# Two Mamba scans on one core: one GpSimd product for each pair, softplus' correction moved from VectorE to ScalarE and TensorE, gating in place

## The chip, the cores and the metric

The kernel runs on one core of one Trainium2 chip. The metric is the device time of one execution in microseconds (us); the time before is the median of three runs, 3107.72 us (3107.16 to 3108.42). TensorE is PE in the profile (its weight loads PEld), VectorE DVE, ScalarE ACT, GpSimd POOL, SyncE SP. PSUM is the memory that TensorE writes and ScalarE and VectorE read; SBUF is the working memory of all engines.

## The reference, cut to what matters

Four layers with residuals are applied to an image of 2 x 128 x 56 x 56: an agent attention, a 3x3 convolution, a mixture of experts, and a layer with two Mamba scans, one along each row of 56 positions and one against it. The change touches the last layer alone (and one buffer of the step that leads to it).

```python
def _mamba(x, in_w, conv_w, conv_b, xproj_w, dt_w, dt_b, Alog, Dp, out_w):
    xi, z = jnp.split(x @ in_w.T, 2, axis=-1)
    xc = jax.nn.silu(conv_b + sum((xp[:, k:k + L, :] * conv_w[:, k] for k in range(K))))
    dt, Bm, Cm = jnp.split(xc @ xproj_w.T, [DT_RANK, DT_RANK + D_STATE], axis=-1)
    dt = jax.nn.softplus(dt @ dt_w.T + dt_b)
    A = -jnp.exp(Alog)
    def step(h, inp):                      # 16 states for each of 256 channels
        dA = jnp.exp(dt_l[:, :, None] * A)
        h = dA * h + (dt_l * u_l)[:, :, None] * B_l[:, None, :]
        y = jnp.einsum('bds,bs->bd', h, C_l)
    y = (ys + xc * Dp) * jax.nn.silu(z)
    return y @ out_w.T
fwd = _mamba(xs, ...); bwd = _mamba(xs[:, ::-1, :], ...)[:, ::-1, :]
y = layernorm(jnp.concatenate([fwd, bwd], axis=-1) @ fuse_w.T)
x = x + y
```

## The kernel before, in words

**Blocks, halves and units.** The function mamba_pair cuts the 2 x 3136 positions into 14 blocks of 448 (8 rows). A block has a forward and a backward half (f and b); each half holds 256 channels x 16 states, worked as 8 pairs of units, 16 units in all. One unit is a tile of 128 partitions x 896. So a block is 32 units, and the main loop runs over 14 x 32 = 448 units, one loop step for each.

**One step of the loop**, in program order for every engine:

- `decay` of the next unit: two ScalarE exponentials (line 1820) write dA to PSUM. There are two dA buffers, so the decay of unit n+1 waits until the scan of unit n-1 is done.
- The fetches, ScalarE copies out of PSUM that belong to work booked one step earlier.
- `push` of the unit three ahead: one GpSimd product dBu = dtu2 * B (line 1831, 128 x 896), into one of four dBu buffers.
- `scan` (line 1853): the VectorE recurrence h = dA * h + dBu. After the second unit of a pair, h is multiplied by C: by GpSimd for pairs 0, 3, 6 of f and 0, 3 of b (line 1859, 128 x 1792), by VectorE for the other eleven pairs of the block (line 1862), which then wait for c_ps.
- `close`, when a half is finished: yv = y * zs, the gating by VectorE (line 1879).
- `read_out` (line 1841): TensorE spreads a row of C over partitions, into c_ps, in the single PSUM bank "c".
- `collect` (line 1873): TensorE sums the states of an earlier unit into y. A half's first collect also writes the skip term (line 1869).
- What `book` has put on this step.

**Bookings.** While the units of block n-1 are scanned, block n is prepared. The steps of that preparation are counted from the first unit of block n-1: steps 0 to 15 lie beside its f half, 16 to 31 beside its b half, and steps 32 on are already beside block n's own f half. The order on each engine is the program's (a manual schedule). The line that chooses a PSUM bank is the tag: "mm" or "c", one bank each, so that a matmul group of a tag waits until ScalarE has fetched the group before it. Among the bookings are, for block n: `norm` 6, `f.conv` 7 and 8, silu 10 and 18 (each with two loads of ScalarE's table), `b.conv` 12, `f.low` 15, `f.step` 17 and 20, `f.softplus` 22 (bank "c") and 24, `f.weigh` 25, `f.gate(0)` 26, `f.send_steps` 27, `b.step(0)` 27, `b.softplus` 32 and 33 (both bank "c"), `f.gate(1)` 33, `b.gate(0)` 35, `b.weigh` 38. And for the finished block: `fuse` 36, `measure` 38, `root` and `newton` 39.

**Softplus** is log(1 + exp(-|v|)) + max(v, 0), with a correction for the rounding of 1 + e. For each half and each m of two: `step` lets TensorE write v to dt_ps, and four ScalarE operations follow (lines 1765 to 1769), the last of which writes w = 1 + e back to that bank. `error` (VectorE, line 1775) forms (w - 1) - e. `log` (ScalarE, line 1780) takes ln w into sp_u. `softplus` (line 1785) has TensorE add three terms, ln w, minus the correction and max(v, 0), in sp_ps, and a ScalarE copy (line 1786) brings the sum to dt. `weigh` (line 1793) multiplies it by xc into the buffer of sp_u, and `send_steps` (line 1808) spreads dtu and dt by DMAs from SP's queue to dtu2 and dt2, as the units need them.

Of the kernel before, what the change touches and what calls it, by code (L numbers as in the profile page):

```python
# [8 lines left out]
F32 = mybir.dt.float32  # L9
AF = mybir.ActivationFunctionType  # L10
ALU = mybir.AluOpType
# [6 lines left out]
P = 128  # L18
# [3 lines left out]
BLK = 448  # L22
# [1509 lines left out]
def mamba_pair(net, out, wts, combine):  # L1532
# [5 lines left out]
    tc, nc, a = net.tc, net.nc, net.a  # L1538
# [5 lines left out]
    ways, ln_w, ln_b, both, minus, pads = (  # L1544
        wts.ways,
        wts.ln_w,
        wts.ln_b,
        wts.both,
        wts.minus,
        wts.pads,  # L1550
    )
    with ExitStack() as ctx:
# [7 lines left out]
        def gathered(name):  # L1560

            if name == "g0":
                g = work.tile([P, 2, 2, BLK], F32, name=name, tag="h", bufs=4).rearrange("p m r t -> p (m r t)")
            else:
                g = work.tile([P, 2, BLK], F32, name=name, tag="dBu", bufs=4).rearrange("p r t -> p (r t)")
            return g[:T, :512]

        def wide_bank(name):
# [121 lines left out]
        class Half:  # L1690
# [25 lines left out]
            def gate(self, m):  # L1716
                pm = mm("gate_ps")
                if m == 0:
                    self.zs = work.tile([P, 2, BLK], F32, name="zs", tag=f"zs{self.w.d}", bufs=1 if self.w.d == "f" else 2)
                nc.tensor.matmul(  # L1720
                    rows(pm[:, :BLK]),
                    self.w.gate[:, m, :],
                    self.blk.xn[:, :, K - 1 : K - 1 + HW],
                    start=True,
                    stop=True,
                )
                return lambda: nc.scalar.copy(self.zs[:, m, :], pm[:, :BLK])
# [25 lines left out]
            def step(self, m):  # L1753
                pm = mm("dt_ps")
                nc.tensor.matmul(pm[:, :BLK], self.w.dt_t[:, m, :], self.lo[:R, :], start=True, stop=True)
                if m == 0:
                    self.e = work.tile([P, 2, BLK], F32, name="sp_e", tag="sp_e", bufs=1)
                    self.dt = work.tile([P, 2, BLK], F32, name="dt", tag="dt")
                    self.ue = {}
                self.ue[m] = pm[:, :BLK]  # L1760
                bias = self.w.dt_b[:, m : m + 1]

                def fetch():
                    e = self.e[:, m, :]
                    nc.scalar.activation(e, pm[:, :BLK], AF.Abs, bias=bias)
                    nc.scalar.activation(self.dt[:, m, :], pm[:, :BLK], AF.Relu, bias=bias)
                    nc.scalar.activation(e, e, AF.Exp, scale=-1.0)

                    nc.scalar.activation(pm[:, :BLK], e, AF.Identity, bias=1.0)

                return fetch

            def error(self, m):
                e = self.e[:, m, :]
                nc.vector.scalar_tensor_tensor(e, self.ue[m], 1.0, e, ALU.subtract, ALU.subtract)

            def log(self, m):
                if m == 0:
                    self.u = work.tile([P, 2, BLK], F32, name="sp_u", tag="sp_u", bufs=1)
                nc.scalar.activation(self.u[:, m, :], self.ue[m], AF.Ln)  # L1780

            def softplus(self, m):
                pm = mm("sp_ps")
                for n, (mat, v) in enumerate(((net.ident, self.u), (minus, self.e), (net.ident, self.dt))):
                    nc.tensor.matmul(pm[:, :BLK], mat, v[:, m, :], start=n == 0, stop=n == 2)
                return lambda: nc.scalar.copy(self.dt[:, m, :], pm[:, :BLK])

            def weigh(self, m=None):
# [10 lines left out]
            def send_steps(self, m=None):  # L1799

                some = slice(0, 2) if m is None else slice(m, m + 1)
                if not m:
                    self.dt2 = work.tile([P, 2, 2, BLK], F32, name="dt2", tag="dt2")
                    self.dtu2 = work.tile([P, 2, 2, BLK], F32, name="dtu2", tag="dtu2")
                for to, src, queue in ((self.dtu2, self.dtu, nc.sync), (self.dt2, self.dt, nc.sync if m is None else nc.gpsimd)):
                    for s in range(2):
                        for r in range(2):
                            queue.dma_start(to[s * H : (s + 1) * H, some, r, :], src[r * H : (r + 1) * H, some, :])
# [15 lines left out]
                        scale=self.w.A[:, j, 2 * m + r : 2 * m + r + 1],  # L1824
                    )

            def push(self, u):
                j, m = self.unit(u)
                shape = [P, 2, BLK]
                self.dBu[u] = work.tile(shape, F32, name="dBu", tag="dBu", bufs=4)  # L1830
                nc.gpsimd.tensor_tensor(  # L1831
                    self.dBu[u], self.dtu2[:, m], self.B[:, j, :].unsqueeze(1).to_broadcast(shape), ALU.mult
                )

            def read_out(self, u):
# [7 lines left out]
            def scan(self, u):  # L1843

                j, m = self.unit(u)
                if m == 0:
                    self.hc[j] = work.tile([P, 2, 2, BLK], F32, name="h", tag="h", bufs=4)
                h = self.hc[j]
                hf, bf = (v.rearrange("p r t -> p (r t)") for v in (h[:, m], self.dBu[u]))
                af = self.dA[u][:, : 2 * BLK]  # L1850
                if self.w.d == "b":
                    hf, af, bf = hf[:, ::-1], af[:, ::-1], bf[:, ::-1]
                nc.vector.tensor_tensor_scan(hf, af, bf, 0.0, ALU.mult, ALU.add)  # L1853
                if m == 1:
                    shape = [P, 4, BLK]
                    h4 = h.rearrange("p m r t -> p (m r) t")
                    if self.by_pool(u):
                        c = self.C[:, self.w.pooled.index(j), :].unsqueeze(1).to_broadcast(shape)
                        nc.gpsimd.tensor_tensor(h4, h4, c, ALU.mult)  # L1859
                    else:  # L1860
                        c = self.c_ps[:, :BLK].unsqueeze(1).to_broadcast(shape)
                        nc.vector.tensor_tensor(h4, h4, c, ALU.mult)  # L1862
# [12 lines left out]
                    )  # L1875

            def close(self):
                self.yv = work.tile([P, 2, BLK], F32, name="yv", tag=f"yv{self.w.d}", bufs=1)
                nc.vector.tensor_mul(self.yv, self.y[:, :, :BLK], self.zs)

        def silu(inputs, gates):
# [11 lines left out]
        def book(step, *stages, tag="mm", late=0):  # L1893

            agenda.setdefault(step, []).extend((stage, tag, late) for stage in stages)

        for n, blk in enumerate(blocks):

            f, b = blk.ways
            at = STEPS * (n - 1)  # L1900
            if n == 0:
# [7 lines left out]
                book(at + 9, lambda f=f: f.step(1), tag="c", late=1)  # L1909
                book(at + 9, f.send_low)  # L1910
                for m in range(2):
                    book(at + 10 + m, lambda f=f, m=m: f.error(m))
                    book(at + 10 + m, lambda f=f, m=m: f.log(m))
                    book(at + 11 + m, lambda f=f, m=m: f.softplus(m), tag=("mm", "c")[m])
                    book(at + 12 + m, lambda f=f, m=m: f.weigh(m))
                    book(at + 12 + m, lambda f=f, m=m: f.send_steps(m))
# [4 lines left out]
                book(at + 19, lambda b=b: silu(b, None))  # L1921
                for m in range(2):
                    book(2 + 3 * m, lambda b=b, m=m: b.step(m))
                    book(3 + 3 * m, lambda b=b, m=m: b.error(m))
                    book(4 + 3 * m, lambda b=b, m=m: b.log(m))
                    book(7 + m, lambda b=b, m=m: b.softplus(m))
                book(0, b.low)
# [2 lines left out]
            else:  # L1930
# [8 lines left out]
                book(at + 17, f.send_low)  # L1939
                book(at + 17, lambda f=f: f.step(0))  # L1940
                book(at + 18, lambda b=b, g=before.ways[1]: silu(b, g))
                book(at + 19, lambda f=f: f.error(0))
                book(at + 19, lambda f=f: f.log(0))
                book(at + 20, lambda f=f: f.step(1))
                book(at + 21, lambda f=f: f.error(1))
                book(at + 22, lambda f=f: f.log(1))
                book(at + 22, lambda f=f: f.softplus(0), tag="c")
                book(at + 23, b.low)
# [2 lines left out]
                book(at + 26, lambda f=f: f.gate(0))  # L1951
                book(at + 27, lambda b=b: b.step(0))
                book(at + 27, f.send_steps)
                book(at + 28, lambda b=b: b.error(0))
                book(at + 28, lambda b=b: b.log(0))
                book(at + 29, lambda b=b: b.step(1))
                book(at + 31, lambda b=b: b.error(1))
                book(at + 31, lambda b=b: b.log(1))
                book(at + 32, lambda b=b: b.softplus(0), tag="c")
                book(at + 33, lambda f=f: f.gate(1), late=1)  # L1960
                book(at + 33, lambda b=b: b.softplus(1), tag="c")
                book(at + 33, b.send_low)
                book(at + 35, lambda b=b: b.gate(0))
                book(at + 38, b.weigh)
                book(at + 43, b.send_steps)
                book(at + 46, lambda b=b: b.gate(1), late=1)
# [43 lines left out]
                pass  # L2010
        with tc.manual_schedule(engines={E.PE, E.Activation, E.DVE, E.Pool, E.SP}):
            units[0][0].decay(0)
            for h, u in units[:3]:
                h.push(u)
            for n, (h, u) in enumerate(units):
                if n + 1 < len(units):
                    who, i = units[n + 1]
                    who.decay(i)
                fetch(n)
                if n + 3 < len(units):  # L2020
                    who, i = units[n + 3]
                    who.push(i)
                h.scan(u)
                if done:
                    done.pop().close()
# [117 lines left out]
```

## Time and profile before

| | us |
|---|---|
| median of three runs | 3107.72 |
| profiled execution, its own time | 3104.97 |
| its span | 3103.2 |
| first to last scan (448 units, 14 blocks) | 1736.9 to 3075.4 |
| one block in between, from the third unit pair of a b half to the next (2476.72 to 2571.45) | 94.73 |
| in that block: POOL, DVE, PE, ACT busy | 92.22, 89.88, 85.03, 69.85 |

How to read it: the Mamba part takes 1338 of the span's 3103 us. POOL has the most busy time in it and DVE nearly as much, but both sit idle in places. A share of busy time does not say which of them sets the pace; the waits do. In the timeline, a line gives the start, the length, the engine, the code line, the operation and, in brackets, how long the engine sat idle before it and what ended that.

### The profile page before, as it was taken

Reading aid. Unit: us, or ns where it says so; the run is one execution under the profiler, and the core shown is the slowest. Engines: PE = TensorE matmul, PEld = TensorE weight load, DVE = VectorE, ACT = ScalarE, POOL = GpSimd, SP = SyncE. Lnnn points to the kernel's source line nnn. Section 1 sums busy time; section 2 is a strip of 40 time slices with the busy share of each in tenths; the row PEclk is TensorE's granted clock in tenths of the full one; section 3 lists DMA queues with packets and bytes.
Section 4 is the critical chain, followed back from the end, with each engine's and each line's share of the span. In section 5 each row is a group of like instructions: output and inputs, shape, how many; then the busy total and the mean of one; then the engine's idle time right before and its main releaser. Section 6 shows DMA issues by size and latency. Waiting matters only on the chain. (4 is left out here: it accounts for less than half of the span.)

```text
span 3103.2 us, 34608 instructions
## 1 busy us (share of the span) xinstructions
PE 2821.9 (91%) x12964; PEld 1076.6 (35%) x12964; DVE 2224.9 (72%) x2033; ACT 1758.6 (57%) x2634; POOL 1499.1 (48%) x801
## 2 busy tenths in 40 slices
PE   7999999999898899999996789989899998889885
PEld 3333333332334444444443322333323333233321
DVE  5879999999887111111112699999999999999996
ACT  5778788877641011111111577776677767777764
POOL 3000100100511000000003699999999999999995
PEclk9999999999998899999997888999889899999987
DMA  1000000000011878787773553454444535444440
GB/s 54 1 1 1 1 1 1 1 1 1 1 38 43 317 280 323 286 314 301 298 309 104 115 102 81 91 106 90 93 89 84 112 81 113 90 84 91 95 101 8
DMA packets 133271, 333.65 MB, mean 108 GB/s; under 512 B 20228, under 2 KB 90340, under 8 KB 129492
## 3 DMA queue, kind: packets, MB, share of 16 engines
q1 hardware_dynamic: 111104, 303.96, 34.0%
q0 software_dynamic: 5520, 15.62, 1.6%
q10 hardware_dynamic: 16452, 11.61, 1.2%
q8 instruction: 106, 1.74, 0.2%
q14 instruction: 89, 0.73, 0.1%
HBM read 262.56 MB, written 17.20 MB: 90 GB/s over the span
## 5 line engine op out<-in xcount | busy, mean ns | idle before, releaser
L1831 POOL TENSOR_TENSOR dBu<-dtu,Bs 128x896 f32<-128x896 f32 x448 | 943.6, 2136 | 51.7 <-DVE h L1853 39.1
L1853 DVE TENSOR_TENSOR_SCAN h<-dA,dBu 128x896 f32<-128x896 f32 x448 | 878.7, 2006 | 59.7 <-ACT dA L1820 47.4
L620 ACT ACTIVATE ex<-sc 128x896 f32<-128x896 f32 (+1 forms) x700 | 602.7, 917 | 124.4 <-PE sc L617 113.3
L627 DVE TENSOR_TENSOR ex_sum<-ex_sum,ex 128x1792 f32<-128x1792 f32 (+1 forms) x238 | 492.5, 2069 | 35.2 <-ACT ex L620 21.2
L1873 PE MATMUL y<-h,both 128*64 128x448 f32 x1792 | 469.1, 625 | 16.1 <-POOL h L1859 14.9
L617 PE MATMUL sc<-q,k 32*128 32x448 f32 (+1 forms) x2800 | 403.5, 587 | 3.6 <-ACT ex L620 2.9
L1341 PE MATMUL h_ps<-w,xs_c 128*128 128x512 f32 x896 | 393.4, 597 | 10.3 <-issue 10.3
L1820 ACT ACTIVATE dA<-dt,f_A 128x448 f32<-128x448 f32 x448 | 284.4, 637 | 107.0 <-DVE h L1853 76.4
L635 PE MATMUL av<-ex,va 128*32 128x448 f32 (+1 forms) x2800 | 334.3, 552 | 0.1
L1862 DVE TENSOR_TENSOR h<-h,c_ps 128x1792 f32<-128x1792 f32 x154 | 311.3, 2021 | 26.2 <-PE c_ps L1841 11.5
L582 POOL TENSOR_TENSOR a_e<-a_e,a_inv 112x784 f32<-112x784 f32 x14 | 41.6, 2974 | 583.2 <-ACT ex L620 394.5
L1820 ACT ACTIVATE dA<-dt,b_A 128x448 f32<-128x448 f32 x448 | 283.8, 636 | 66.6 <-DVE h L1853 53.2
L1345 DVE TENSOR_TENSOR he<-h_ps,sg 128x512 f32<-128x512 f32 x56 | 38.5, 691 | 381.8 <-PE h_ps L1341 344.3
L1289 POOL DMA_INDIRECT xr<-xd,whom x28 | 28.1, 1003 | 534.8 <-PE xr_ps L1331 490.1
L1859 POOL TENSOR_TENSOR h<-h,Cs 128x1792 f32<-128x1792 f32 x70 | 279.3, 3990 | 2.5 <-DVE h L1853 2.4
L1841 PE MATMUL c_ps<-low,ident 40*64 40x448 f32 x616 | 172.9, 643 | 89.6 <-DVE h L1862 67.5
L1341 PEld LDWEIGHTS h_ps<-w,xs_c 128*128 128x128 f32 x896 | 169.0, 191 | 218.5 <-issue 202.8
L1873 PEld LDWEIGHTS y<-h,both 128*64 128x64 f32 x1792 | 116.7, 150 | 320.0 <-issue 250.7
L617 PEld LDWEIGHTS sc<-q,k 32*128 32x128 f32 (+1 forms) x2800 | 137.7, 181 | 230.0 <-issue 135.2
L1362 PE MATMUL o_ps<-w,ht 128*128 128x512 f32 x448 | 197.2, 592 | 0.4 <-ACT ht L1357 0.4
L1344 ACT ACTIVATE sg<-h_ps 128x512 f32<-128x512 f32 x56 | 33.4, 597 | 256.0 <-PE h_ps L1341 256.0
L1364 ACT ACTIVATE ot<-o_ps,share 128x512 f32<-128x512 f32 x28 | 19.3, 688 | 278.9 <-PE o_ps L1362 278.9
(334 smaller groups left out, 3057.9 us busy)
## 6 DMA issues: line engine op xcount, KB each, us to landing
w<-in_L_conv_w_dram SPq DMA_DIRECT2D x28, 4096.0 KB, 19.4
w<-in_L_conv_w_dram SPq DMA_DIRECT2D x28, 2048.0 KB, 10.2
Bs<-far SPq DMA_DIRECT2D x56, 896.0 KB, 8.6
dtu<-sp_u SPq DMA_DIRECT2D x108, 224.0 KB, 3.9
dt<-dt SPq DMA_DIRECT2D x108, 224.0 KB, 5.2
Cs<-far SPq DMA_DIRECT2D x140, 112.0 KB, 7.3
os<-ot ACTq DMA_DIRECT2D x28, 256.0 KB, 7.8
xd<-xt SPq DMA_DIRECT2D x14, 224.0 KB, 2.7
```

The source lines that it names most:

```text
L617: nc.tensor.matmul(sc[:size, j, :BLK], self.m.k[rows, at : at + size], self.q[rows, :], start=True, stop=True)
L620: nc.scalar.activation(ex[:size, 2 * g : 2 * g + 2, :], sc[:size, :, :BLK], AF.Exp, scale=scale)
L627: nc.vector.tensor_add(self.total[g][:size], self.total[g][:size], ex[:size])
L635: nc.tensor.matmul(self.av[rows, :BLK], self.m.va[:size, i, rows], self.ex[i][:size, h, :], start=i == 0, stop=i == STEPS - 1,)
L1341: nc.tensor.matmul(h_ps, xc[:, q, :], w1[:, q, f0 : f0 + 512], start=q == 0, stop=q == 3)
L1362: nc.tensor.matmul(o_ps, ht[:, i, :], w2[:, i, :], start=i == 0, stop=i == nj - 1)
L1820: nc.scalar.activation(self.dA[u][:, r * BLK : (r + 1) * BLK], self.dt2[:, m, r, :], AF.Exp, scale=self.w.A[:, j, 2 * m + r : 2 * m + r + 1],)
L1831: nc.gpsimd.tensor_tensor(self.dBu[u], self.dtu2[:, m], self.B[:, j, :].unsqueeze(1).to_broadcast(shape), ALU.mult)
L1853: nc.vector.tensor_tensor_scan(hf, af, bf, 0.0, ALU.mult, ALU.add)
L1859: nc.gpsimd.tensor_tensor(h4, h4, c, ALU.mult)
L1862: nc.vector.tensor_tensor(h4, h4, c, ALU.mult)
L1873: nc.tensor.matmul(self.y[r * H : (r + 1) * H, m, :BLK], both, self.hc[j][:, m, r, :], start=False, stop=j == PAIRS - 1)
```

## The change

Three edits, all in mamba_pair:

- `push` now forms the products of a whole pair in one GpSimd operation of 128 x 1792, four units ahead at every second step, into one of three buffers of twice the size.
- `error` is gone. `log` has a second ScalarE operation that writes w - 1 into a free part of the tile dtu2 (which is now allocated in `step`), and TensorE's sum has four terms: e, minus (w - 1), ln w, max(v, 0).
- `close` writes its product over zs, and yv is no tile of its own. The f half's zs gets two buffers and the b half's one.

Three bookings move: `b.log(0)` from step 28 to 29, `b.step(1)` from 29 to 30, `b.gate(0)` from 35 to 38. The second buffer of the experts' gather before the Mamba part shares the dBu tiles, so there are three of them instead of four.

```diff
             def log(self, m):
                 if m == 0:
                     self.u = work.tile([P, 2, BLK], F32, name="sp_u", tag="sp_u", bufs=1)
                 nc.scalar.activation(self.u[:, m, :], self.ue[m], AF.Ln)
+                nc.scalar.activation(self.dtu2[:, m, 0, :], self.ue[m], AF.Identity, bias=-1.0)
-            def error(self, m):
-                e = self.e[:, m, :]
-                nc.vector.scalar_tensor_tensor(e, self.ue[m], 1.0, e, ALU.subtract, ALU.subtract)
             def softplus(self, m):
                 pm = mm("sp_ps")
-                for n, (mat, v) in enumerate(((net.ident, self.u), (minus, self.e), (net.ident, self.dt))):
-                    nc.tensor.matmul(pm[:, :BLK], mat, v[:, m, :], start=n == 0, stop=n == 2)
+                terms = (
+                    (net.ident, self.e[:, m, :]),
+                    (minus, self.dtu2[:, m, 0, :]),
+                    (net.ident, self.u[:, m, :]),
+                    (net.ident, self.dt[:, m, :]),
+                )
+                for n, (mat, v) in enumerate(terms):
+                    nc.tensor.matmul(pm[:, :BLK], mat, v, start=n == 0, stop=n == 3)
                 return lambda: nc.scalar.copy(self.dt[:, m, :], pm[:, :BLK])
-            def push(self, u):
-                j, m = self.unit(u)
-                shape = [P, 2, BLK]
-                self.dBu[u] = work.tile(shape, F32, name="dBu", tag="dBu", bufs=4)
+            def push(self, j):
+                shape = [P, 4, BLK]
+                self.dBu[j] = work.tile([P, 2, 2, BLK], F32, name="dBu", tag="dBu", bufs=3)
                 nc.gpsimd.tensor_tensor(
-                    self.dBu[u], self.dtu2[:, m], self.B[:, j, :].unsqueeze(1).to_broadcast(shape), ALU.mult
+                    self.dBu[j].rearrange("p m r t -> p (m r) t"),
+                    self.dtu2.rearrange("p m r t -> p (m r) t"),
+                    self.B[:, j, :].unsqueeze(1).to_broadcast(shape),
+                    ALU.mult,
                 )
             def close(self):
-                self.yv = work.tile([P, 2, BLK], F32, name="yv", tag=f"yv{self.w.d}", bufs=1)
+                self.yv = self.zs
                 nc.vector.tensor_mul(self.yv, self.y[:, :, :BLK], self.zs)
...
-                    self.zs = work.tile([P, 2, BLK], F32, name="zs", tag=f"zs{self.w.d}", bufs=1 if self.w.d == "f" else 2)
+                    self.zs = work.tile([P, 2, BLK], F32, name="zs", tag=f"zs{self.w.d}", bufs=2 if self.w.d == "f" else 1)
...
...
-                book(at + 28, lambda b=b: b.error(0))
-                book(at + 28, lambda b=b: b.log(0))
-                book(at + 29, lambda b=b: b.step(1))
-                book(at + 31, lambda b=b: b.error(1))
+                book(at + 29, lambda b=b: b.log(0))
+                book(at + 30, lambda b=b: b.step(1))
                 book(at + 31, lambda b=b: b.log(1))
...
-                book(at + 35, lambda b=b: b.gate(0))
+                book(at + 38, lambda b=b: b.gate(0))
...
-            for h, u in units[:3]:
-                h.push(u)
+            for h, u in units[:4:2]:
+                h.push(u // 2)
...
-                if n + 3 < len(units):
-                    who, i = units[n + 3]
-                    who.push(i)
+                if n % 2 == 0 and n + 4 < len(units):
+                    who, i = units[n + 4]
+                    who.push(i // 2)
```

## The prediction

> **What bounds the kernel now.** I read the page's costliest groups first, then the waits of DVE and POOL over eleven blocks (1928.3 to 2979.9 us), then the timeline of one block. From the page:
>
> ```profile
> L1831 POOL TENSOR_TENSOR dBu<-dtu,Bs 128x896 f32<-128x896 f32 x448 | 943.6, 2136 | 51.7 <-DVE h L1853 39.1
> L1853 DVE TENSOR_TENSOR_SCAN h<-dA,dBu 128x896 f32<-128x896 f32 x448 | 878.7, 2006 | 59.7 <-ACT dA L1820 47.4
> L1859 POOL TENSOR_TENSOR h<-h,Cs 128x1792 f32<-128x1792 f32 x70 | 279.3, 3990 | 2.5 <-DVE h L1853 2.4
> ```
>
> POOL is the busiest, but its idle time ends with a scan of DVE, and DVE's with a dA of ACT. The waits over eleven blocks (total us, times, longest):
>
> ```profile
> DVE h L1853 <- ACT dA L1820: 38.3, 34, 2.0
> DVE h L1862 <- PE c_ps L1841: 5.0, 11, 0.9
> POOL dBu L1831 <- DVE h L1853: 27.3, 32, 1.9
> ```
>
> No scan waits for POOL there; POOL waits for DVE to free a dBu buffer. So the pace is DVE's chain with ACT's and PE's delays in it. In the block of 94.73 us, DVE:
>
> ```profile
> 2476.72 3.94 DVE L1853 TENSOR_TENSOR_SCAN h<-dA,dBu 128x896 f32<-128x896 f32 x2 [1.98 <-ACT dA L1820]
> 2493.30 3.93 DVE L1853 TENSOR_TENSOR_SCAN h<-dA,dBu 128x896 f32<-128x896 f32 x2
> 2506.34 3.94 DVE L1853 TENSOR_TENSOR_SCAN h<-dA,dBu 128x896 f32<-128x896 f32 x2 [0.49 <-ACT dA L1820]
> 2520.88 2.02 DVE L1862 TENSOR_TENSOR h<-h,c_ps 128x1792 f32<-128x1792 f32 x1 [0.22 <-PE c_ps L1841]
> 2548.25 2.02 DVE L1853 TENSOR_TENSOR_SCAN h<-dA,dBu 128x896 f32<-128x896 f32 x1 [0.84 <-ACT dA L1820]
> ```
>
> PE, the sums of softplus (two records each matmul) and the convolution:
>
> ```profile
> 2483.02 1.02 PE L1785 MATMUL sp_ps<-sp_u,ident 128*128 128x448 f32 x2
> 2489.67 1.02 PE L1785 MATMUL sp_ps<-sp_u,ident 128*128 128x448 f32 x2
> ...
> 2512.46 1.02 PE L1785 MATMUL sp_ps<-sp_u,ident 128*128 128x448 f32 x2 [1.40 <-DVE h L1862]
> 2516.72 1.02 PE L1785 MATMUL sp_ps<-sp_u,ident 128*128 128x448 f32 x2
> 2519.87 0.97 PE L1841 MATMUL c_ps<-low,ident 40*64 40x448 f32 x4 [0.62 <-ACT dt L1786]
> ...
> 2533.40 3.31 PE L1703 MATMUL conv_ps<-pad,f_conv_t 128*128 128x448 f32 x8
> ```
>
> ACT, behind the second of the f sums, and behind the DMAs:
>
> ```profile
> 2492.23 0.53 ACT L1786 COPY dt<-sp_ps 128x448 f32<-128x448 f32 x1 [1.55 <-PE sp_ps L1785]
> 2492.66 1.31 ACT L1820 ACTIVATE dA<-dt,b_A 128x448 f32<-128x448 f32 x2
> ...
> 2504.50 0.54 ACT L1780 ACTIVATE sp_u<-dt_ps 128x448 f32<-128x448 f32 x1 [3.81 <-DMA dtu<-sp_u]
> ```
>
> **B products in pairs.** Five products in a row take 10.52 us, 2.104 each, 4.21 a pair. The nearest row for one of 128x1792 is the C product (3.99, the next starts 3.95 behind it). 224 x (4.21 - 3.95) = 58 us less of POOL. Cover: POOL's slack, so on the path 0 (without that slack the 58 us would count, which is a rival below). The nearest threat is the first pair of an f half, which must wait for dtu's DMAs. POOL's weigh would end near 2496.8; the log came 6.6 after it (2497.9 to 2504.5), so the DMAs are in at 2503.4, the product at 2507.4, and its scan is wanted at 2511.4: 4 us to spare. At the very start a scan waits for 3.96 instead of 2.14, and for both DMAs; block 0's waits for ACT and PE (1.2, 0.4, 0.3, 2.0) take most of that back.
>
> **The correction, one block.** DVE loses 4 operations of 0.61 (56 x 613 ns = 34.3 us in all). ACT gains 4 of about 0.53 (the Ln row is 534 ns, the copy of 1 + e 548), PE 4 matmuls, 0.75 us each (the sums' terms start 0.75 apart). Where each lies:
>
> *f sums.* error(0) stood in the 1.98 us wait before step 20, for ACT's second table load: gain 0. error(1) and its wait gave DVE 0.7. But PE runs from 2483.02 to the second sum without a gap, so the two added matmuls bring that sum's copy 1.5 later, 2492.23 to 2493.73. The dA behind it then ends at 2495.5 instead of 2494.0. The scan that needs it ran at 2495.25; it could be 0.7 earlier, and will be 0.25 later. The DVE gain turns into a wait: **+0.25**.
>
> *b half, steps 28 to 31.* error(0) 0.52 goes. The log behind the DMAs blocked the dA of step 30 (0.49); booked a step later it blocks that of step 31, which is due at 2507.4 and done at 2505.7: gain 0.49. Step(1), booked one later too, now stands behind c_ps of step 30 in PE's queue, and its four ACT operations and the two of log(1) end near 2511.8; the dA of step 33 behind them is done at 2513.1 and due at 2513.35, so nothing queues, with 0.25 to spare. SP's and POOL's orders do not change there. Error(1) falls in the next item. With a POOL that weighs 1.1 earlier, h * c of step 31 ends at 2511.45 instead of 2512.40: **-0.95** (the +0.25 is in it; without it -1.2).
>
> *b sums.* From the freed bank "c" (2512.4) to c_ps and h * c (2520.88), PE goes sum, collect, gate, sum without a gap, then copy, c_ps. Two matmuls more: 8.5 becomes 10.0. DVE needs 7.9 for its four scans and loses error(1)'s 0.54, so its wait grows from 0.22 to about 2.1. h * c comes at 2511.45 + 10.0 = 2521.4: **+0.55 against before**, all items so far together.
>
> **b.gate(0) later.** At step 35 PE did it while it waited for DVE. At 38 it stands between fuse and f's conv(0), which share the bank "mm": gate 0.75, its fill 0.3 and ACT's copy 0.53 must pass before conv(0), while the collects that filled 2530.24 to 2533.40 cover the gate but not the copy. Conv(0) starts 0.73 later, and with it conv(1), the silu and the dA that the scan at 2548.25 already waits 0.84 for: **+0.73**, in full. Its bounds: 0, if the convolution's copies find slack in ACT, and 1.3. Gating in place itself: the same row (1083 ns), 0; the copy into the b half's one zs must wait for fuse, which PE has finished by then (2530.24). The gather's third instead of fourth buffer: the first is free 4.3 us after its issue (1668.94 to 1673.23), and with three it would be issued again after 8.0 (1676.98), 0.
>
> **The sum.** 0.55 + 0.73 = 1.28 us a block. The next 23 us, to the scan after the second silu, are a chain behind this one and move along. Blocks prepared beside another: 13. 13 x 1.28 = 16.6; the last block's two waits for POOL (1.1) go; the start and block 0 I take as 0, between -4 (DVE no longer waits 2.0 and 1.9 for two corrections there) and +4. On the profiled run 3104.97 (span 3103.2 and 1.8 around it) that is 3120.5; that run lies 2.75 below the median, on which I put it: **3123**.
>
> **Two rules of the Trainium skill.** PE's clock first. In the block shown it is granted 0.57 over 2499.72 to 2503.72, behind a PE wait of 1.22 us; in another block 0.50 from 2308.7 to 2322, which reaches the b sums. The page TensorE: Matmul & The Clock Gate (Part 1) gives half rate only after an idle window of about 3.4 us; no PE gap that long stands before these stretches, so the measurement decides that shorter gaps do. By the rule the sums would always run at full clock and the sum above stands; by the rows some blocks pay up to 1.5 us more. Second, the page ScalarE: Activation LUTs (Rules for kernel authors) gives additions to VectorE, not ScalarE, which speaks against this edit; here the subtraction on DVE takes 613 ns and the same size on ACT 548, so the operation is no dearer, and the loss I expect comes from the queues.
>
> **Rivals.** *DVE's saving counts* (faster): PE's sums have slack that I do not see, c_ps and the f copy come as before, and DVE keeps 0.7 + 0.52 + 0.49 + 0.54 = 2.25 a block, less the gate's 0.73: 13 x 1.5 = 20 us, 3088; without the gate 3078. It decides if the c_ps wait stays under 0.7. For it: ACT is idle for 25 of the 94.73 us, so a copy that comes later can find room; against it: PE's rows without gaps. Chance 0.20. *POOL was the pace*: the 58 us come in part, 3060; against it is every wait of the steady blocks. 0.05. *One delay of the three is covered*: 13 x 0.5 or less, 3105 to 3113: 0.13. *Half clock in the sums*: 1.5 us more in most blocks, 3140: 0.12. *The wider product binds*: a scan waits about 2 us for POOL once in each half, only if the 4 us of margin are gone, 3150: 0.03. *My forecast*: 0.47.
>
> **How the numbers follow.** About 0.2% (6 us) is what a measurement tells from no change. Slower by more: 0.47 + 0.12 + 0.03 = 0.62. Within: 0.13. Faster: 0.25. The range runs from the faster rival with little left out, 3082, to the half-clock case and a bit, 3143; about 0.05 lies below (POOL) with part of the first rival, 0.05 above. The forecast's own range is 3112 to 3134.
>
> **What would show it.** Right: DVE's wait for c_ps grows from 5.0 us in eleven blocks to over 15; the ACT copy of sp_ps waits longer; the wait of 0.84 becomes about 1.6; POOL idles some 7 us a block, still waiting for DVE or DMAs; block period near 96. Wrong: c_ps waits unchanged with DVE idle down (first rival), scans that wait for dBu (wide product), or a PE clock that differs much from 0.93 in such a block.

## The result and the profile after

The changed kernel takes **3200.22 us** (median; 3198.64 to 3200.38) beside 3107.44 (3103.13 to 3108.42) for the kernel before: ratio 1.030, 95% interval 1.0282 to 1.0318. The forecast was 3123, slower by 15; the sign came true, the size did not: 93 us. The profiled execution has a span of 3196.9 us and a mean granted TensorE clock of 0.922 (before: 3103.2 and 0.937).

The page's busy times and groups (busy us, mean ns of one, then the idle time ahead of the group and what ended it):

```profile
PE 2908.0 (91%) x13076; PEld 1109.3 (35%) x13076; DVE 2200.0 (69%) x1977; ACT 1779.2 (56%) x2690; POOL 1461.7 (46%) x577
L1857 DVE TENSOR_TENSOR_SCAN h<-dA,dBu 128x896 f32<-128x896 f32 x448 | 883.0, 2008 | 120.0 <-ACT dA L1822 108.4
L1832 POOL TENSOR_TENSOR dBu<-dtu,Bs 128x1792 f32<-128x1792 f32 x224 | 903.0, 4057 | 76.2 <-DVE h L1857 41.8
L1866 DVE TENSOR_TENSOR h<-h,c_ps 128x1792 f32<-128x1792 f32 x154 | 311.3, 2021 | 60.1 <-PE c_ps L1845 45.0
```

Every engine that was to be relieved was relieved: POOL's products take 40 us less (903.0 for 943.6; the forecast had 58, with 3.95 a pair where the busy time gives 903.0 / 224 = 4.03), VectorE has 25 us less to do. And VectorE's waits are longer by far more: the scans waited 59.7 us before and 120.0 now, of which 108.4 for a dA of ScalarE. One block, from a scan of step 20 to the next (VectorE's timeline, only the instructions that waited; the waits in brackets):

```profile
2222.59 4.05 DVE L1857 TENSOR_TENSOR_SCAN h<-dA,dBu 128x896 f32<-128x896 f32 x2 [2.50 <-ACT dA L1822]
2241.31 2.02 DVE L1857 TENSOR_TENSOR_SCAN h<-dA,dBu 128x896 f32<-128x896 f32 x1 [0.81 <-ACT dA L1822]
2261.21 3.94 DVE L1857 TENSOR_TENSOR_SCAN h<-dA,dBu 128x896 f32<-128x896 f32 x2 [1.87 <-ACT dA L1822]
2265.80 2.02 DVE L1857 TENSOR_TENSOR_SCAN h<-dA,dBu 128x896 f32<-128x896 f32 x1 [0.66 <-ACT dA L1822]
2270.50 2.02 DVE L1866 TENSOR_TENSOR h<-h,c_ps 128x1792 f32<-128x1792 f32 x1 [2.68 <-PE c_ps L1845]
2283.46 0.87 DVE L1641 BATCH_NORM_STATS2 ln_st<-ln_y 112x6 f32<-112x128 f32 x4 [2.04 <-ACT ln_y L1635]
2287.12 0.16 DVE L1657 SCALAR_TENSOR_TENSOR ln_t<-ln_mv,ln_ps 112x4 f32<-112x4 f32 x1 [0.61 <-ACT ln_ps L1649]
2301.80 3.94 DVE L1857 TENSOR_TENSOR_SCAN h<-dA,dBu 128x896 f32<-128x896 f32 x2 [1.92 <-ACT dA L1822]
```

Against the block of the kernel before there are waits where there were none: at the scans of steps 27 (2241.31), 33 (2261.21; the expectations below call it the scan of step 32) and 35 (2265.80), at the LayerNorm's ln_st and ln_t, and a long one at h * c of step 35 (2270.50). TensorE in the same block says why. In these rows a number in brackets is idle time, and each matmul has two records; a sum's term takes 0.75 us of the queue at full clock and 1.5 or more at half:

```profile
2251.48 1.76 PE L1845 MATMUL c_ps<-low,ident 40*64 40x448 f32 x4 [3.35 <-DVE h L1866]
2254.86 1.86 PE L1755 MATMUL dt_ps<-low,b_dt_t 8*128 8x448 f32 x2
2259.84 1.86 PE L1788 MATMUL sp_ps<-sp_e,ident 128*128 128x448 f32 x2
...
2269.48 0.97 PE L1845 MATMUL c_ps<-low,ident 40*64 40x448 f32 x4 [0.62 <-ACT dt L1789]
2272.57 1.76 PE L1845 MATMUL c_ps<-low,ident 40*64 40x448 f32 x4 [1.22 <-DVE h L1866]
2274.26 3.35 PE L1873 MATMUL y<-xc,f_skip 128*128 128x448 f32 x4
```

Two idle times, 3.35 us ahead of the c_ps of step 30 and 1.22 ahead of that of step 36, and behind each of them matmuls that take about twice as long: c_ps 1.76 for 0.97, dt_ps 1.86 for 1.01, the skip product 3.35 for the 1.77 of before. The granted clock goes with it. In the rows of stretches of time, after the busy times of PE, PEld, DVE, ACT and POOL, the third number from the end is the granted clock (then DMA share and GB/s):

```profile
2248.20:2250.76 2.56, 0.00 (x0) 0.00 (x0) 2.46 (x2) 1.88 (x4) 1.21 (x1) 1.00 1.08 211
2253.32:2255.88 2.56, 2.56 (x6) 0.64 (x6) 2.46 (x3) 1.28 (x2) 2.56 (x2) 0.50 0.00 0
2258.44:2261.00 2.56, 2.56 (x6) 0.75 (x3) 0.89 (x1) 2.50 (x5) 2.56 (x2) 0.50 0.33 112
2273.80:2276.36 2.56, 2.56 (x5) 1.17 (x4) 2.56 (x2) 0.84 (x2) 1.52 (x1) 0.50 0.00 0
```

0.00 of PE in the first row is the idle time; then the clock is 0.50 for some ten microseconds (2251.4 to 2261.6), and again behind the second gap (2271.9 to 2278.7). Both gaps come from the change. In the kernel before, dt_ps of b.step(1) lay in the first (at step 29; now at 30, behind the c_ps that waits) and b.gate(0)'s matmul in the second (at step 35; now at 38).

The blocks of one execution differ, and that is a test by itself. The gap of 1.22 us ahead of the c_ps of step 36 stands in all 13 blocks. In 8 of them the clock behind it is 0.50 and ln_st waits 2.0 to 2.1 us; in the other 5 the clock stays at 1.00 and ln_st does not wait. From h * c of step 35 to the scan of step 44 it is 31.3 to 31.7 us in the 8 (less in the last block, which has no successor) and 28.5 in the 5. The gap ahead of the c_ps of step 30 is 3.35 us in 7 blocks; in the other 6 it begins at half clock and is 1.8 to 2.7 us long.

There is a third place, which the change did not open. A gap of some 2.8 us ahead of the c_ps of step 20, beside ScalarE's table loads, stands in the kernel before too, and behind it the clock is 0.50 in every block. Mostly it is back at 1.00 before the f sums. In 3 of the changed kernel's 13 blocks it is not; in one of these:

```profile
2011.87 1.76 PE L1845 MATMUL c_ps<-low,ident 40*64 40x448 f32 x4 [2.82 <-DVE h L1866]
...
2020.32 4.75 PE L1877 MATMUL y<-h,both 128*64 128x448 f32 x12
2025.00 1.56 PE L1788 MATMUL sp_ps<-sp_e,ident 128*128 128x448 f32 x2
```

Here the clock is 0.50 from 2009.0 to 2026.1 (in the block shown above only from 2217.3 to 2224.1). The scan of step 27 then runs 4.0 us later than in the other blocks and h * c of step 35 some 2.5 later. The kernel before has one such block, where scan 27 is 2.5 late.

That gives two theories for the experiments. **H**: the two gaps bring TensorE to half clock, and the late sums, skip and fuse cost the time. **W**: the work itself costs all of it, the four added matmuls, ScalarE's four added operations and the gate's late place, at whatever clock.

### The profile page after: what moved, and what is told of

It reads as the page before. It is cut to its first block, busy times and chain, and to the rows that moved or that the text cites. A ratio compares the mean times of both kernels' runs of the same rounds, so it can differ in the third digit from the quotient of the medians.

```text
span 3196.9 us, 34467 instructions
## 1 busy us (share of the span) xinstructions
PE 2908.0 (91%) x13076; PEld 1109.3 (35%) x13076; DVE 2200.0 (69%) x1977; ACT 1779.2 (56%) x2690; POOL 1461.7 (46%) x577
## 5 line engine op out<-in xcount | busy, mean ns | idle before, releaser
L1857 DVE TENSOR_TENSOR_SCAN h<-dA,dBu 128x896 f32<-128x896 f32 x448 | 883.0, 2008 | 120.0 <-ACT dA L1822 108.4
L1832 POOL TENSOR_TENSOR dBu<-dtu,Bs 128x1792 f32<-128x1792 f32 x224 | 903.0, 4057 | 76.2 <-DVE h L1857 41.8
L1877 PE MATMUL y<-h,both 128*64 128x448 f32 x1792 | 478.5, 630 | 13.7 <-POOL h L1863 9.9
```

What stands on the lines that cost most here:

```text
L1832: nc.gpsimd.tensor_tensor(self.dBu[j].rearrange("p m r t -> p (m r) t"), self.dtu2.rearrange("p m r t -> p (m r) t"), self.B[:, j, :].unsq ...
L1877: nc.tensor.matmul(self.y[r * H : (r + 1) * H, m, :BLK], both, self.hc[j][:, m, r, :], start=False, stop=j == PAIRS - 1)
```

## The experiments

Times are medians; the kernel before, on the same chip each time, took 3104.95 to 3109.67, and the ratios are to it.

### Parts of the change alone, undone, or given more work

*gate_late*: the gating part alone, on the kernel before.

```
-  zs: bufs=1 if self.w.d == "f" else 2      self.yv = work.tile(...)
+  zs: bufs=2 if self.w.d == "f" else 1      self.yv = self.zs
-  book(at + 35, lambda b=b: b.gate(0))
+  book(at + 38, lambda b=b: b.gate(0))
```

> The kernel before with one part of the change alone: outputs gated in place (f's zs two buffers, b's one, no yv) and b.gate(0) booked at step 38 instead of 35. Theory H (idle TensorE, then half clock): in the changed kernel TensorE waits 1.22 us at the c_ps of step 36, where gate(0) stood before, and the skip product, the collects and fuse behind it run at 0.50, so the LayerNorm's rows come some 3 us late. Then this edit alone costs about 3 us in most of 13 blocks: some 3140 to 3150, with the wait of ln_st for ln_y near 2 us. Theory W (it is the work that was moved and added, at any clock): only the 0.73 us a block that the gate's own matmuls and copy take between fuse and conv: about 3117, ln_st not waiting.

Measured 3153.44, ratio 1.0141 (1.0117 to 1.0165): 3 us above H's range, and far from W's 3117. VectorE's waits over eleven blocks (1920 to 2980 us; us in all, times, longest) hold what the edit made, and TensorE's rows the way to it:

```profile
DVE ln_st L1641 <- ACT ln_y L1635: 24.0, 11, 2.3
DVE ln_t L1657 <- ACT ln_ps L1649: 6.7, 11, 0.6
```

```profile
2153.41 1.75 PE L1841 MATMUL c_ps<-low,ident 40*64 40x448 f32 x4 [1.22 <-DVE h L1862]
2155.10 3.35 PE L1869 MATMUL y<-xc,f_skip 128*128 128x448 f32 x4
2158.38 1.76 PE L1873 MATMUL y<-h,both 128*64 128x448 f32 x4
```

Neither wait was there before. LayerNorm waits 2.8 us a block for a TensorE at half clock, here in all eleven blocks, and the scan of step 44 waits 1.07 more (0.84 before, 1.91 now), which is the gate's own place.

*corr_only*: the correction part alone, on the kernel before, with log and step one later.

```
-  error() on VectorE; three terms in softplus()
+  nc.scalar.activation(self.dtu2[:, m, 0, :], self.ue[m], AF.Identity, bias=-1.0); four terms
-  b.log(0) at 28, b.step(1) at 29
+  b.log(0) at 29, b.step(1) at 30
```

> The kernel before with the correction alone: no operation on VectorE, a second operation of ScalarE in log, four terms in each sum, and b.log(0) and b.step(1) one step later, at 29 and 30. Gating, the gate's place and the half products are those of before. Theory H: dt_ps of step(1), one step later in TensorE's queue, leaves TensorE idle for about 3.3 us ahead of the c_ps of step 30, and c_ps, dt_ps and the first sum behind it run at 0.50: about 3.2 us a block more at h * c of step 35, so 3107 + 13 x (3.2 + 0.25) = some 3150. Theory W: two terms more in the b sums, at full clock, as in the forecast: +0.55 a block, about 3115.

Measured 3148.40, ratio 1.0131 (1.0108 to 1.0153): H's number again. The wait for c_ps is 27.6 us in eleven blocks (5.0 before), the 3.35 us gap and the half clock behind it are in the trace, and LayerNorm doesn't wait. The two parts alone cost 48 and 43 us, together 92 of the change's 93.

*undo_steps*: the changed kernel with `b.log(0)` back at 28 and `b.step(1)` at 29.

> The changed kernel with b.log(0) and b.step(1) back at steps 28 and 29; everything else as changed. Theory H: TensorE has dt_ps to do where it was idle for 3.35 us, the half clock ahead of the b sums goes, and about 3.2 us of 7.2 a block come back: 3200 - 13 x 3.2 = 3158. Theory W: the four matmuls and the four operations of ScalarE are all still there, and the log stands behind the DMAs again: 3200, or up to 6 more.

Measured 3161.79 (1.0172, 1.0149 to 1.0194), 38 less than the changed kernel, near H's 3158 and far from W's. The gap isn't gone: dt_ps now waits 2.3 us there for ScalarE's log, whose second operation it must await, and the clock falls behind that wait too, but dt_ps starts earlier. LayerNorm waits less as well (0.8 us in most blocks), so not all of the 38 is the first gap's.

*fill35* and *fill29*: the changed kernel with **more** for TensorE to do. One unread gate product at step 35, or four products of a zero matrix with xc, added to y, at step 29.

```
+  book(at + 35, lambda b=b: b.idle35())      # matmul of gate's operands into bank mm, not read
```
```
+  book(at + 29, before.ways[1].idle29)       # 4 x matmul(y, zero, xc, start=False, stop=False)
```

> The changed kernel with one matmul more in each prepared block: at step 35, where gate(0) stood, TensorE makes a product of the same operands into the same bank that nobody reads; gate(0) stays at 38. It is more work (13 x 0.75 us of TensorE) and takes nothing away. Theory H: TensorE is idle for 0.2 us instead of 1.2 there, keeps full clock through skip and fuse, and the kernel gets faster by some 3 us in most blocks: 3160 to 3170. Theory W: 3200 or a few us more.

> The changed kernel with four matmuls more in each prepared block at the end of step 29, ahead of the c_ps of step 30 (a zero matrix times xc, added to the block's y, which it leaves as it is): 3 us more work for TensorE, put where it is idle for 3.35 us. Theory H (the idle time ahead of that c_ps brings the half clock): c_ps, dt_ps and the first sum run at 1.00, dt_ps ends some 2 us earlier, the scan of step 32 waits about 0 instead of 1.87 us for dA, and the wait for c_ps falls from 2.67 to about 1: some 3 us a block, near 3160. Theory W (the work itself): nothing gained, 3200 or up to 10 more.

Measured 3183.68 (1.0241, 1.0221 to 1.0262) and 3151.82 (1.0130, 1.0107 to 1.0153). Useless work makes the kernel 17 and 48 us faster. W, which has only more to pay, is refuted as the cause of the 93 us. fill35 gives half of what H expected. LayerNorm no longer waits at all, but in 5 of 11 blocks of the profiled changed kernel it had not waited either (12.3 us of waits in 6 blocks). And the third place takes some back: the f sums are late in 6 of fill35's 13 blocks, every second one, where the changed kernel has 3. fill29 gives more than the 40 that was expected; its f sums are late in one block.

*fill_both*: both fillings.

> Both fillings of TensorE's idle time in the changed kernel: four products with zero at step 29 and one unread gate product at step 35. Theory H: both episodes of half clock go, the gains add (17 us measured for step 35, some 40 for step 29): about 3143, with what is left over the kernel before being the gate's later place (1.07 us a block), the added terms and scan 20. Theory W: no gain over fill35 alone, 3184 or more.

Measured 3129.96 (1.0066, 1.0049 to 1.0083), 70 us below the changed kernel and 13 below H's 3143. VectorE's waits in one block:

```profile
2295.07 4.05 DVE L1873 TENSOR_TENSOR_SCAN h<-dA,dBu 128x896 f32<-128x896 f32 x2 [2.50 <-ACT dA L1838]
2332.54 5.85 DVE L1873 TENSOR_TENSOR_SCAN h<-dA,dBu 128x896 f32<-128x896 f32 x3 [0.73 <-ACT dA L1838]
2339.72 2.02 DVE L1882 TENSOR_TENSOR h<-h,c_ps 128x1792 f32<-128x1792 f32 x1 [1.33 <-PE c_ps L1861]
2368.20 7.77 DVE L1873 TENSOR_TENSOR_SCAN h<-dA,dBu 128x896 f32<-128x896 f32 x4 [1.92 <-ACT dA L1838]
2391.39 2.02 DVE L1873 TENSOR_TENSOR_SCAN h<-dA,dBu 128x896 f32<-128x896 f32 x1 [2.50 <-ACT dA L1838]
```

*gate1_at35*: no work more or less; `book(at + 33, f.gate(1), late=1)` becomes `book(at + 35, f.gate(1))`.

> The changed kernel with f.gate(1) moved from step 33 to step 35 (its copy still at 36): no work is added or left out. Its matmuls leave the place between the two b sums and stand where TensorE is idle for 1.22 us. Theory H: ln_st no longer waits (2.65 us in 9 of 11 blocks) and the c_ps of step 34 comes 0.9 us earlier: 3200 - 24 - 12 = about 3164. Theory W: only the 0.9 us a block: about 3188.

Measured 3158.96 (1.0162, 1.0145 to 1.0179): 41 less by moving one matmul into the gap, and H's number, a little better. The wait for LayerNorm is gone, and the wait at c_ps is 1.91 instead of 2.68. The second is not the gap's doing: the matmul also left its old place between the b sums, for which the expectation has 12 us under either theory.

### The paired products

*pairs_gate*: the changed kernel with the correction edit undone, that is gate_late with paired products.

> The changed kernel without its correction edit: B products of a pair in one operation, outputs gated in place with b.gate(0) at 38, but error() on VectorE, three terms in the sum and log/step at 28 and 29 as before. Beside gate_late (3153) it differs in the paired products alone. If these cost and bring nothing, as forecast: 3150 to 3157, scans not waiting for GpSimd. Rival P (the longer product blocks the h * C products and the weighing behind it): slower than 3157, with the wait of the first scans of a half for GpSimd.

Measured 3160.52 (1.0167, 1.0150 to 1.0184); gate_late is at 1.0141 (1.0117 to 1.0165). The intervals overlap: pairs cost between nothing and some 0.5%, and no gain is seen. In the traces twelve steady blocks take 1187.9 us in both, and the first LayerNorm row comes 3.3 us later with pairs: what they cost is at the start. Paired products alone, with separate outputs of the gating, were not run.

### What is left, and whether the clock counts by itself

*corr_fill29*: corr_only with the four products with zero at step 29.

> The kernel before with the correction edit (as in corr_only, 3148) and four products with zero at step 29, ahead of the c_ps of step 30. Theory H (idle time, then half clock): nearly all that corr_only lost comes back, since its 43 us are the 3.3 us a block of TensorE's late b sums: 3100 to 3112. Theory W (the terms that were added to the sums, the operations of ScalarE): 3148 and some us for the fillers.

Measured 3115.26 (1.0020, 1.0008 to 1.0031). 33 of corr_only's 43 us come back, not all: H's range was 3 us too low. In its block c_ps still waits 2.09 us, which at full clock is the price of two terms more in each sum (the forecast had 2.1). In the profiled execution the first three blocks lose another 3.4 to 3.9 us each at the third place, the f sums; the others are at 95.6.

*before_fill*: the kernel before with one product with zero in each of its own three gaps of steps 27 to 32.

```
+  book(at + 27, ... b.idle(1)), book(at + 29, ... b.idle(1)), book(at + 31, ... b.idle(1))
```

> The kernel before with one product with zero at each of TensorE's three idle places of steps 28 to 32 (the gaps of 1.22, 1.42 and 1.40 us). Theory H: half clock costs only where somebody waits for TensorE's result next, and in the kernel before nobody does (0.22 us for c_ps, 0.49 at scan 30, in part for a DMA): no change to 8 us faster, 3099 to 3107. Rival C (the mean clock sets the time, wherever it is lost): some 2% higher clock in a fifth of the block, 20 us or more faster.

Measured 3113.13 (1.0015, 1.0006 to 1.0025): no gain, rather some 5 us lost. Its mean clock rose from 0.937 to 0.943, and the time with it. As a test of rival C it is a weak one: two of the three gaps are filled, but ahead of dt_ps of step 29 a gap of 2.3 to 4.0 us is left in every block, with a clock of 0.50 to 0.66 behind it, so the mean clock rose by 0.6% only. fill18 below, which has the higher clock and the longer time, speaks more clearly against C. H stands in its narrow form: half clock costs where an engine on the path waits for the result.

*sum34_pairs* and *sum34_half*: a try at a kernel faster than both, with paired products and with halves.

```
-  book(at + 33, lambda f=f: f.gate(1), late=1);  book(at + 33, lambda b=b: b.softplus(1), tag="c")
+  book(at + 33, lambda f=f: f.gate(1));          book(at + 34, lambda b=b: b.softplus(1))
-  book(at + 38, lambda b=b: b.gate(0))
+  book(at + 42, lambda b=b: b.gate(0))
+  (the products with zero at 29; sum34_half: on corr_only, so gate(0) from 35 to 42)
```

> The changed kernel with four products with zero at step 29, the second b sum at step 34 in bank mm instead of step 33 in bank c (so that the c_ps of step 34 no longer stands behind both sums, and the sum fills the idle 1.2 us), f.gate(1)'s copy one step sooner, and b.gate(0) at 42, behind the f convolutions. From the block of fill_both (96.3 us) the wait for c_ps (1.33) and the gate's 1.07 go: 93.9 us a block, 3130 - 31 = about 3099, faster than the kernel before by some 8 us. If bank mm, which now passes gate(1), the sum and fuse in a row, holds up fuse: ln_st waits, 3115 or more.

> The same moves (products with zero at 29, second b sum at 34 in mm, b.gate(0) at 42) and the correction edit on the kernel before, with half products and separate outputs of the gating. If paired products bring nothing: the same time as sum34_pairs within 4 us. If the pair products cost what pairs_gate lay over gate_late (7 us): about 3092.

Measured 3114.57 (1.0015, 1.0005 to 1.0025) and 3122.12 (1.0038, 1.0023 to 1.0052): neither is faster than the kernel before. The 3099 that was expected was missed by 15, and not for the reason allowed for: ln_st does not wait. sum34_pairs' blocks of 94.3 to 95.6 us are level with the 95.2 of before; its start is 6 us later and one block, with late f sums, has 98.8. What the gate's move won at step 44 is paid behind it: from there to the next scan of step 20 it is 24.4 us instead of 23.2. The halves are slower by 7.6, neither level with the pairs nor faster. VectorE's waits for POOL over eleven blocks, of sum34_half and then of sum34_pairs, show a part of the cause:

```profile
DVE h L1862 <- POOL dBu L1840: 9.1, 19, 1.0
DVE h L1863 <- POOL dBu L1838: 6.1, 3, 2.6
```

With the correction gone from VectorE and the wait at c_ps down to 9 us in eleven blocks, scans begin to wait for POOL's half products, 19 times in steady blocks. That is 3.0 us more than with pairs. Most of the other 9 us between these two executions is a second block with late f sums (some 4 us) and 3.4 us in the last block.

*start_split*, *fill_start* and *fill18*, each on fill_both, and *all_of_it*, on sum34_pairs with the three together.

```
start_split:  h.push(u // 2, parts=2 if u == 0 else 1)          # the first pair as two of 128x896
fill_start:   book(6, lambda f=f: f.zeros(f, 4))                # block 0, ahead of its first b sum
fill18:       book(at + 18, ... g.spare(f, 16))                 # 16 x 64 columns, unread, ahead of step 20
```

> fill_both (3130) with the very first product of block 0's f half made as two of 128x896. If the wider first product costs the start: the first scan comes 2 us or more earlier (it waits for one half's DMAs and 2.1 us instead of for both and 4 us), 3125 to 3128. If what follows in block 0 takes it back (c_ps comes when it came): 3130.

> fill_both (3130) with four products with zero more, once, at step 6 of block 0, where TensorE is idle for 3.41 us ahead of the first b sum. If the half clock makes that sum late: its four terms take 3.0 instead of 6.1 us, the wait of 7.80 us for c_ps falls to about 4.7, 3127. If it is the terms themselves: 3130 or a little more.

> fill_both (3130) with TensorE kept busy by sixteen products of 64 columns at step 18 of each block, in the 2.82 us ahead of the c_ps of step 20, written to columns of y's bank that nobody reads. If the half clock behind that gap makes the f sums late: scan 27 no longer waits 0.81 us for dA, 13 x 0.8 = 10 us, 3120. If the two added terms do: TensorE runs without a gap to the second f sum anyway, only its start moves, and 3130 stays.

> sum34_pairs (3115) with the three: first product in two, products with zero at step 6 of block 0 and at step 18 of each block. If all three are on the path: 3115 - 3 - 3 - 10 = 3099, faster than the kernel before by some 8 us. If only the ones at the start: 3109, as before.

Measured 3130.86 (1.0061, 1.0047 to 1.0075), 3131.16 (1.0069, 1.0055 to 1.0083) and 3136.13 (1.0094, 1.0078 to 1.0109) beside fill_both's 1.0066, and 3110.40 (1.0008, 0.9999 to 1.0017) for all_of_it. The first two moved nothing that can be measured: fill_start's wait for c_ps in block 0 is 4.95 us where fill_both has 6.64. The first scan of the profiled executions lies at 1736.7 to 1738.7 in the six kernels with half products, at 1740.7 to 1748.5 in the ten that form the first pair in one operation, and at 1745.7 and 1734.8 in the two that split it. So the pairs do start later, but what the split gains at the start can't be settled this way. fill18 kept the clock at 1.00 from step 18 to behind the f sums in 6 of its 13 blocks; in one of them (stretches as above; its scan of step 20 is at 2300.49):

```profile
2302.50:2305.00 2.50, 2.26 (x12) 0.57 (x8) 2.40 (x3) 2.42 (x5) 2.50 (x1) 1.00 1.03 189
2305.00:2307.50 2.50, 0.78 (x2) 0.49 (x3) 2.50 (x2) 2.44 (x5) 2.50 (x2) 1.00 0.06 12
```

In such blocks it gained nothing: TensorE idles at 2305 for the bank that the first f sum needs, and the wait of 0.81 us at the scan of step 27 stays. That wait is the two added terms. In 6 others the clock falls in that new gap of 1.96 us, ahead of the first f sum, and scan 27 comes 1.7 us later still. fill18 has the highest mean clock of the kernels made on fill_both, 0.965 for 0.953, and is 6 us slower. all_of_it has the same 1.7 us in 7 of its 13 blocks; it is level with the kernel before, and no kernel of this study beats it.

## Why the prediction was right and wrong

The block, cut at the scan of step 20, h * c of step 35, the scan of step 44 and the next scan of step 20, from VectorE's timelines (us). Each row is one block, with f sums that are not late; for the changed kernel one of the 8 in which LayerNorm waits:

| | 20 to h * c(35) | to scan 44 | to next 20 | block |
|---|---|---|---|---|
| before | 44.16 | 27.37 | 23.20 | 94.73 |
| forecast | 44.71 | 28.10 | 23.20 | 96.01 |
| changed kernel | 47.91 | 31.30 | 23.19 | 102.40 |
| gate_late | 43.94 | 31.58 | 23.20 | 98.72 |
| corr_only | 48.07 | 27.36 | 23.19 | 98.62 |
| corr_fill29 | 45.07 | 27.36 | 23.19 | 95.62 |
| fill35 | 47.65 | 28.48 | 23.19 | 99.32 |
| fill_both | 44.65 | 28.48 | 23.19 | 96.32 |

**Right.** The sign. That in the steady blocks nothing waits for POOL, so that 40 us less of it are worth nothing; in sum34_half, where VectorE waits less for c_ps, the half products begin to count. That VectorE's saving turns into waits. +0.25 at the f sums: scan 27 runs at 18.72 us from the scan of step 20 (forecast 18.78) in all but 4 of the 13 blocks, and fill18 shows the two terms as the cause. -0.95 up to h * c of step 31: measured -0.87 (it ends 34.81 behind the scan of step 20, 35.68 before). The last 23 us move along. And fill_both, the change with its gaps filled, has the forecast's block almost row by row: 44.65 for 44.71, 28.48 for 28.10, and 3129.96 us for 3123. The sum of the queues was good; it was a sum for a TensorE at full clock.

**Wrong: the b half's term.** "+0.55 against before" at h * c of step 35, behind the sums. Measured: +3.75. The step that failed is the sentence that step(1), one later, "now stands behind c_ps of step 30 in PE's queue", and that the dA of step 33 behind it is done 0.25 before it is due, "so nothing queues". Measured: the scan of step 33 waits 1.87 us for that dA. The forecast asked what waits behind the moved matmul and not what TensorE does in the place that it left: nothing, for 3.35 us, and then c_ps, the collects, dt_ps and the first term of the sum at half clock. ScalarE, with four operations to do, waits 2.05 us for dt_ps (0.47 in fill_both); the scan of step 33 and the sums come late with them.

**Wrong: the gate's term.** "+0.73, in full", bounds 0 to 1.3. Measured +3.93. The text names the cover itself: "at step 35 PE did it while it waited for DVE". Taking that work away was priced at nothing. It cost 2.82 us (31.30 less fill35's 28.48), LayerNorm's wait behind a half-clock skip and collects, in 8 of the 13 blocks; the gate's own place cost 1.11 (28.48 less 27.37), which is the term as it was meant, within its bounds.

**Wrong: the half clock as a rival.** It had 0.12 and 1.5 us a block, only in the sums. In the block of the table it has two places and 6 us: 102.40 less 96.32. The forecast had the rows that show a gap of 1.22 us ahead of 0.50, and used them to make the clock a matter of luck between blocks, not of what the change does to the gaps. Luck between blocks there is too: the third place, 3 blocks of 13, and the 5 blocks in which the second gap costs nothing.

**Wrong: the start.** 0 between -4 and +4. Measured: the scan of step 20 of block 0 comes at 1816.61 after 1808.45, 8.2 us late. The first scan is 5.3 of that (1742.16 after 1736.90): the first product waits for the DMAs of both halves and starts at 1738.16 instead of 1734.74, and it lasts 4.0 instead of 2.1. The forecast had both, and let block 0's waits "take most of that back". They do not: the wait for c_ps behind block 0's own b sum grows from 3.37 to 7.80 us. That sum has four terms instead of three, and here it runs at half clock, behind a gap of 3.41 us; the kernel before has 2.98 us of idle time there and full clock behind it.

**The rest of the time.** The first LayerNorm row comes at 1875.26 after 1863.78, 11.5 late: 8.2 of the start and 3.3 of the first block prepared beside another. The 12 blocks from there on take 102.00 us each on average, 95.20 before: 81.5. The last one adds 0.9, and that is the 94 us between the spans.

## What to carry to other kernels

Before a matmul is moved, look at what TensorE does in the place it leaves: where it fills a wait, moving it away can halve the clock for some microseconds behind (7 to 17 in the stretches read here), and that is paid wherever a copy, a scan or a LayerNorm waits for those matmuls. The quickest test is more work: products with zero in the suspected gap; if the kernel gets faster, the gap was a cause, and useful work moved there (gate1_at35: 41 us, 12 of them expected from the place it left) is the mend. Count over all blocks, not in one: here the same gap cost 2.8 us in 8 blocks and nothing in 5. Relieving an engine is worth something only if its work ends a wait; here 40 us less on GpSimd and 25 on VectorE brought no gain in time, since VectorE waits for ScalarE and TensorE.

## What was not expected of the hardware

How short a gap can be enough, and that its length alone does not decide. In the traces of the kernel before, the changed kernel and gate_late (1860 to 2980 us), counting all gaps of 0.99 us and more that began at a clock of 1.00, the granted clock from 0.5 to 2.5 us after the gap was:

| idle time of TensorE | gaps | still 1.00 | below 0.65 |
|---|---|---|---|
| 0.99 to 1.00 us | 35 | 35 | 0 |
| 1.22 to 1.23 us | 44 | 10 | 33 |
| 1.34 to 1.52 us | 7 | 4 | 1 |
| 2.69 to 3.35 us | 43 | 0 | 43 |

In fill18, 6 of 12 gaps of 1.96 us left the clock at 1.00. What the traces do show is a fixed grid in time. Read from the rows of stretches, the clock of the changed kernel fell at 2251.40, came back at 2261.64, fell at 2271.88 and came back at 2278.70; the last three come 3, 6 and 8 times 3.413 us after the first. All 64 changes of the clock in that trace from 1900 to 2960 us lie on this grid to within 0.02 us, and so do, each on a grid of the same step, the 53 of the kernel before and the 66 of gate_late. So a gap of 1.22 us costs clock or not by where it lies on the grid, and the block times agree with it: three blocks in a row of 102.40 to 102.42 us are 30 steps each, and gate_late's 12 blocks are 98.99 us on average, which is 29. How much idle time in a step brings the fall is not settled: the step that ended at 2271.88 held 1.1 us, and others with as much left the clock at 1.00.

The Trainium skill's page TensorE: Matmul & The Clock Gate advises (Why this matters for your kernels) no idle gaps of more than about 3 us between bursts, and in Part 1 says that half rate comes after an idle window of some 3.4 us that runs freely. The step of 3.413 us on a grid of its own agrees with such a window. That it must be idle from end to end does not: 1.22 us were enough in three of four cases here. By the page's rule the second gap would cost no clock, and gate_late would lose no more than the gate's 1.1 us a block.
